# Attention and mixture of experts on one core: expert biases moved into the weights, and the softmax exponentials moved to ScalarE in front of the transposes

## The chip, the core and the metric

The kernel runs on one core of a Trainium2 chip. The core has five engines that run side by side, each through its own list of instructions in a fixed order: TensorE (PE, matmuls and transposes into PSUM), VectorE (DVE), ScalarE (ACT), GpSimd (POOL) and SyncE (SP, here an issuer of DMAs). They meet through semaphores. The metric is the device time of one execution in microseconds (us). Most executions of one kernel agree within 0.3%.

## What is computed

One transformer layer on x of shape 8 x 512 x 256 (eight batches), all in float32: causal attention with 16 heads of width 16, a layer norm, then a mixture of 16 experts of width 176 of which each token uses 6, and one shared expert of width 352, and a second layer norm.

```python
qkv = x @ w_qkv                                   # 16 heads of 16
scores = where(causal, q @ k.T / 4, -1e10)
x = layernorm(x + (softmax(scores) @ v) @ w_out)  # no gain, no offset
probs = softmax(x @ gate_w.T)
idx = top_k(probs + gate_b, 6);  c = probs at idx, else 0
y = sum over e of c[e] * ((silu(x @ w1[e].T + b1[e]) * (x @ w3[e].T + b3[e])) @ w2[e].T + b2[e])
z = (silu(x @ ws1.T + bs1) * (x @ ws3.T + bs3)) @ ws2.T + bs2
out = layernorm(x + y + z)
```

The layer norm has no learned gain or offset, so each row of what the experts read sums to zero up to rounding.

## The kernel before

The program is a list of steps ("line" in the code), and TensorE's instructions stand in exactly the order in which the steps write them; the other engines' order is chosen by the scheduler of the framework, by its own estimate of when things are ready, and is fixed in the program. Every step is a function `fn`, then what is `due` from earlier steps, then what is put `beside` it, then a function `behind`.

**Attention.** For a batch `transpose_x`, `project_qk` and `project_v` (L302 to L346) come first. Then there are 16 steps, one for each query tile q of 128 rows (q = 0 to 3), each half m of the heads, and each parity s. A step handles four heads (r = 0 to 3). `front` (L559) issues `scores` of step i and `turn_weights` of step i - 1; `back` (L566) issues `weighted_v` of step i - 2.

- `scores` (L348): TensorE computes four score tiles of 128 x (q+1)*128 into the four "sc" buffers of PSUM (L357). DVE adds the mask, scales by -0.25 and takes the row minimum of that, which is minus the row maximum, into `nb` (L368; a second short instruction reads the result out). GpSimd writes nb - e over e (L378), so that e holds score minus maximum.
- `turn_weights` (L384): for each key tile k up to q, TensorE transposes the four heads' 128 x 128 blocks into one "ps" buffer (L390), and ScalarE takes the exponential on the way to SBUF (L392, eT).
- `weighted_v` (L396): TensorE multiplies with v2 (L399). v2 holds, per pair of heads, v of the even head, sixteen ones, v of the odd head. A matmul of parity s thus gives, in 32 rows of `po`, sixteen rows of the weighted sum and sixteen of the row sum of the exponentials.
- `normalize` (L407), after both parities: ScalarE and DVE pick the two sums of even and odd heads apart with the masks `par`, a shuffle brings the sums to their partitions, DVE takes the reciprocal and multiplies (L414 to L426).

**Around it.** `finish_tokens` (output projection and layer norm), `transpose_tokens`, `gate` and `place` follow some steps later by `due`. `gate` leaves the routing weights in `cw` (L487); `place` transposes them into `cT` (L500, L501). `send` (L539) scatters token rows to the experts' slots with indirect DMAs that GpSimd issues. `shared_units` (L592) computes the shared expert of the batch before, beside the attention steps; its `collect` ends with a matmul of `cT` against `b2_sb`, which adds the routed b2 by weight and, through a column of ones, the shared bias (L636).

**Experts.** Batches form three groups (2, 4 and 2). `table` and `spread` (L650, L717) find which expert each tile of 128 routed rows belongs to. A unit of `expert_units` (L735) loads a tile of rows (`fetch`), transposes the next tile's rows and the hidden rows of two tiles before into one PSUM tile `tb` (`turn`; L780, L784; ScalarE copies xgT, L787, and hT, L791), multiplies with W1 and W3 of the expert (`up`, L799, `pab`), adds the two biases by one bf16 matmul (L806: a one-hot row `pick` of the tile's expert against `bparts`, each bias split into three bf16 parts by `split_biases`, L218), forms the gated hidden rows on ScalarE and DVE (L815 to L817), and multiplies with W2 (`down`, L826, `py`); ScalarE copies y (L834) and GpSimd issues the scatter of its rows (L835). The units of group 0 stand beside the attention of batches 2 to 6, those of group 1 beside batches 6 and 7 and after, those of group 2 at the end. `combine_units` (L865) adds a token's six rows on DVE and ends with the layer norm.

**Buffers.** PSUM has three pools: "sc" with four buffers, `po` with one, and "ps" with three, which the transposes of the weights, the projections, the gate, the shared expert, `tb`, `pab` and `py` all take in turn; a buffer is free again when its reader (mostly a copy by ScalarE) is done. In the last group every second tile of the units takes "sc" buffers. Loads and stores with fixed or register addresses are all issued by SP, in one order; three fills of spare slots with 2.2 MB each (`xs` from `none`) stand among them early on.

## Time and profile before

The times are 1665.35, 1656.8 and 1660.16 us, median 1660.16. The profile is of one execution, on the slowest core.

| | |
|---|---|
| profiled execution | 1653.36 us, span of the trace 1651.7 us |
| instructions | 30354 |
| mean granted TensorE clock | 0.931 |
| HBM | 75.61 MB read, 79.58 MB written, 94 GB/s |

| stage (us from the start) | PE busy | DVE | ACT | POOL | granted clock | DMA share |
|---|---|---|---|---|---|---|
| 9 to 108, batch 0 | 80.2 | 56.9 | 32.5 | 45.7 | 0.86 | 0.62 |
| 108 to 221, batch 1 | 99.4 | 68.7 | 38.4 | 68.6 | 0.86 | 0.12 |
| 221 to 341, batch 2 | 105.8 | 76.8 | 41.2 | 70.2 | 0.87 | 0.20 |
| 341 to 486, batch 3 | 134.6 | 80.4 | 59.0 | 85.4 | 0.96 | 0.19 |
| 486 to 635, batch 4 | 135.4 | 79.4 | 58.8 | 84.2 | 0.97 | 0.18 |
| 635 to 784, batch 5 | 135.2 | 83.6 | 60.2 | 87.6 | 0.97 | 0.19 |
| 784 to 951, batch 6 | 148.2 | 93.1 | 64.7 | 90.6 | 0.95 | 0.26 |
| 951 to 1197, batch 7 | 223.8 | 108.8 | 99.3 | 115.9 | 0.96 | 0.29 |
| 1197 to 1597, experts | 356.4 | 167.5 | 162.9 | 156.1 | 0.98 | 0.43 |
| 1597 to 1651, last sum | 0 | 31.6 | 0 | 5.1 | | 0.48 |

How to read it: "busy" is the time in us in which an engine ran instructions within the stage. A stage begins with the first q and k projection of its batch (L319). The granted clock is the share of full speed at which TensorE was let run. DMA share is the mean busy share of the core's 16 DMA engines. Lines such as "L378" are lines of the kernel file printed above; "out<-in" names the tiles; "<-" behind an idle time names what ended it. Ends of matmuls are modelled, so their starts are what to go by.

### The profile page before, as it was taken

The page shows a single profiled execution, that of the slowest core. Times are in us where ns is not written, and L with a number is a line of the kernel's source. Part 1 is how long each engine was busy: PE and PEld are TensorE (multiplying, and loading weights), DVE is VectorE, ACT ScalarE, POOL GpSimd, SP SyncE. Part 2 cuts the span into 40 slices and gives each one's busy share as a digit, 9 for nine tenths or more (in the row PEclk, how much of TensorE's full clock was granted, in tenths as well). Part 3 has the DMA queues.
Part 4 walks back from the last instruction along what each step waited for, and adds up shares of the span by engine and source line. Part 5 has one row for each costly group of instructions (what it writes and reads, how often), then busy time and mean ns, then how long its engine had stood idle before and what let it go on. Part 6 is the DMA issues. An engine that isn't in the chain of part 4 may idle for free.

```text
span 1651.7 us, 30354 instructions
## 1 busy us (share of the span) xinstructions
PE 1420.9 (86%) x9204; PEld 958.5 (58%) x9204; DVE 847.4 (51%) x3058; ACT 619.1 (37%) x1637; POOL 814.8 (49%) x1127
## 2 busy tenths in 40 slices
PE   7688998998999999899898998899888899888950
PEld 4454664665755566566555665566565666556740
DVE  4555756655645564556475534445343322675235
ACT  2232332343443343344343433444343343334520
POOL 4367565647465564746565435444545422343320
PEclk9787988998999999999999999999999999999985
DMA  9611102212121121211222324222233431785324
GB/s 259 195 42 41 47 35 92 60 57 67 55 67 54 44 67 47 71 46 63 69 85 72 91 74 134 71 81 84 69 103 103 130 97 45 228 242 163 97 89 131
DMA packets 147497, 151.37 MB, mean 92 GB/s; under 512 B 51215, under 2 KB 122499, under 8 KB 147338
## 3 DMA queue, kind: packets, MB, share of 16 engines
q1 hardware_dynamic: 126474, 96.69, 21.1%
q0 software_dynamic: 20592, 51.96, 8.6%
q8 instruction: 78, 1.28, 0.3%
q14 instruction: 81, 0.66, 0.1%
q10 hardware_dynamic: 272, 0.79, 0.1%
HBM read 75.61 MB, written 79.58 MB: 94 GB/s over the span
## 4 chain that ended last, share of the span: by engine, by line
PE 62%; DVE 14%; POOL 8%; issue 6%; DMA 5%; ACT 3%; another core or an unknown queue 1%; SPq 0%; POOLq 0%; DVEq 0%; ACTq 0%
PE pab L799 14%; PE py L826 10%; PE tp L390 7%; PE sc L357 5%; PE po L399 4%; DVE o L893 3%; PE qk L319 3%; DVE e L368 3%; PE pa L603 3%; PE tb L780 2%; POOL xs L543 2%; PE tb L784 2%; PE spy L629 2%; DMA o<-acc 2%; POOL e L378 2%
## 5 line engine op out<-in xcount | busy, mean ns | idle before, releaser
L835 POOL DMA_INDIRECT ys<-y,yat x237 | 239.1, 1009 | 336.0 <-ACT y L834 298.3
L799 PE MATMUL pab<-we_sb,xgT 128*128 x936 | 338.3, 485 | 14.8 <-DVE h L817 9.2
L378 POOL TENSOR_SCALAR e<-e,nb 128x512 f32<-128x512 f32 (+3 forms) x512 | 272.6, 544 | 156.9 <-DVE nb L368 143.0
L826 PE MATMUL py<-we_sb,hT 88*128 x948 | 252.8, 389 | 25.5 <-ACT hT L791 12.2
L392 ACT ACTIVATE eT<-tp 128x512 f32<-128x512 f32 x320 | 173.7, 599 | 269.0 <-PE tp L390 243.2
L368 DVE CUSTOM_DVE_ANT_0 e<-sc,none 128x512 f32<-128x512 f32 (+3 forms) x512 | 228.2, 479 | 53.7 <-PE sc L357 34.6
L390 PE MATMUL tp<-ident,e 128*128 128x128 f32 x1280 | 200.7, 300 | 49.7 <-POOL e L378 35.4
L826 PEld LDWEIGHTS py<-we_sb,hT 88*128 88x128 f32 x948 | 173.3, 195 | 98.2 <-issue 49.4
L816 DVE SCALAR_TENSOR_TENSOR h<-h,pab 128x176 f32<-128x176 f32 x237 | 79.4, 335 | 289.2 <-ACT h L815 242.5
L543 POOL DMA_INDIRECT xs<-x,idi x192 | 189.6, 987 | 76.9 <-issue 43.5
L390 PEld LDWEIGHTS tp<-ident,e 128*128 128x128 f32 x1280 | 151.1, 150 | 126.6 <-POOL e L378 68.3
L799 PEld LDWEIGHTS pab<-we_sb,xgT 128*128 128x128 f32 x936 | 165.2, 197 | 85.8 <-issue 19.4
L357 PE MATMUL sc<-kT,qT 32*128 32x384 f32 (+3 forms) x1024 | 140.2, 499 | 16.3 <-DVE nb L368 15.7
L815 ACT ACTIVATE h<-pab 128x176 f32<-128x176 f32 x237 | 75.3, 318 | 204.4 <-PE pab L806 165.8
L834 ACT COPY y<-py 128x256 f32<-128x256 f32 x237 | 88.3, 372 | 161.0 <-PE py L826 142.1
L787 ACT COPY xgT<-tb 128x256 f32<-128x256 f32 x234 | 87.2, 373 | 112.9 <-PE tb L784 76.9
L893 DVE SCALAR_TENSOR_TENSOR o<-yg,kept,o 128x256 f32<-128x256 f32 x192 | 94.3, 491 | 43.7 <-DMA o<-acc 23.3
L784 PE MATMUL tb<-ident,h 128*88 128x128 f32 x474 | 93.6, 280 | 19.4 <-DVE h L817 16.9
L780 PE MATMUL tb<-ident,xg 128*128 128x128 f32 x468 | 93.9, 283 | 16.2 <-DVE qT L328 8.9
L399 PE MATMUL po<-eT,v 128*32 128x128 f32 x2560 | 100.2, 283 | 1.5 <-DVE t L423 1.2
L357 PEld LDWEIGHTS sc<-kT,qT 32*128 32x128 f32 x1024 | 60.0, 192 | 58.1 <-DVE nb L368 29.4
L780 PEld LDWEIGHTS tb<-ident,xg 128*128 128x128 f32 x468 | 65.4, 148 | 43.4 <-issue 14.2
(161 smaller groups left out, 1741.4 us busy)
## 6 DMA issues: line engine op xcount, KB each, us to landing
xg<-xs SPq DMA_DIRECT2D x237, 128.0 KB
yg<-ys SPq DMA_DIRECT2D x96, 256.0 KB
we_sb<-in_w SPq DMA_DIRECT2D x6, 1408.0 KB
xs<-none SPq DMA_DIRECT2D x3, 2176.0 KB
xs<-none SPq DMA_DIRECT2D x48, 136.0 KB
x<-in_x SPq DMA_DIRECT2D x8, 512.0 KB
acc<-x SPq DMA_DIRECT2D x32, 128.0 KB
o<-acc SPq DMA_DIRECT2D x32, 128.0 KB
```

The costliest lines, as they stand in the source:

```text
L357: nc.tensor.matmul(sc[:, :n], lhsT=qT[ts(r, 32), m, s, ts(q, P)], rhs=kT[ts(r, 32), m, :n], start=True, stop=True,)
L368: nc.vector.tensor_tensor_reduce(out=e[:, :n], in0=scs[r][:, :n], in1=mask[:, S - n :], scale=-0.25, scalar=BIG, op0=ALU.add, op1=ALU.min, ...
L378: nc.gpsimd.tensor_scalar(e[:, :n], e[:, :n], -1.0, nb[:, r : r + 1], ALU.mult, ALU.add)
L390: nc.tensor.transpose(tp[:, ts(r, P)], es[r][:, ts(k, P)], ident)
L392: nc.scalar.activation(eT, tp, AF.Exp)
L399: nc.tensor.matmul(po[ts(r, 32), m, s, :], lhsT=v2[:, k, 4 * m + r, s : s + 2, :].rearrange("p h i -> p (h i)"), rhs=eTs[k][:, ts(r, P)], ...
L543: d = nc.gpsimd.indirect_dma_start(out=grp.xs, out_offset=bass.IndirectOffsetOnAxis(ap=idi[:, k : k + 1], axis=0), in_=xts[b][:, t, :], in ...
L780: nc.tensor.transpose(tp[:, c, :], xg[:, ts(c, P)], ident)
L799: nc.tensor.matmul(pab, lhsT=xgT[:, c, :], rhs=we_sb[:, ds(e * WE + c * 2 * EH, 2 * EH)], start=(c == 0), stop=False,)
L826: nc.tensor.matmul(py, lhsT=hT[:, c, :], rhs=we_sb[:HC, ds(e * WE + 4 * EH + c * D, D)], start=(c == 0), stop=(c == 1),)
L835: d = nc.gpsimd.indirect_dma_start(out=grp.ys, out_offset=bass.IndirectOffsetOnAxis(ap=st["at", j].bitcast(I32), axis=0), in_=y, in_offset ...
L893: nc.vector.scalar_tensor_tensor(o, y, kept[b][:, t, k : k + 1], o, ALU.mult, ALU.add)
```

## The change

Two things are changed.

First, the biases. The rows that the experts read sum to zero. Adding the same value to all 256 weights of a hidden unit therefore changes nothing. The copy of the transposed rows now adds one at feature 127 and at feature 255 (the last column of the identity matrix as a per-partition bias), so that the product gains the two weights at those features. `shifts` computes for each hidden unit half of (bias - weight 127 - weight 255) and stores it in DRAM, and `shift_weights` adds it to all weights of one expert, in place, for 16 experts in 16 consecutive steps. The matmul with `pick` and `bparts` and its preparation are gone. b2 goes into a row of the weights for the second product: hT keeps a row of ones behind its 88 rows, in two fixed tiles, and the last hidden tile of the shared expert, now one fixed tile, keeps a row of ones behind its 96. The matmul with `cT`, the tiles `cw` and `cT` and their transposes are gone.

Second, the softmax. GpSimd's subtraction is replaced by ScalarE's exponential with the maximum as bias, which also gives the row sums, before the transposes; the copy after the transposes is a plain one. v2 has zeros where it had ones, and both parities accumulate into the same 32 rows of `po`. The row sums' reciprocals are taken on DVE, spread over 16 columns by GpSimd (`over`), transposed by TensorE into the second half of `po`, copied by ScalarE (overT) and multiplied in by DVE.

```diff
+    nc.sync.dma_start(out=ws2_sb[LAST : LAST + 1, NHS - 1, :], in_=b2[E : E + 1, :])
...
+    nc.sync.dma_start(
+        out=wev[HC : HC + 1, :, 4 * EH + D :], in_=b2[:E, :].unsqueeze(0)
+    )
...
-    nc.gpsimd.memset(v2, 1.0)
+    nc.gpsimd.memset(v2, 0.0)
+    hTs = []
+    for i in range(2):
+        t = const.tile([P, 2, P], F32, tag=f"hT{i}", name=f"hT{i}")
+        nc.gpsimd.memset(t, 1.0)
+        hTs.append(t)
+    sh_last = const.tile([P, S], F32, name="sh_last")
+    nc.gpsimd.memset(sh_last, 1.0)
...
-    def split_biases():
+    def shifts():
...
-        for k in range(3):
-            part = three.tile([E, 2, EH], BF16, tag="h", name=f"part_{k}")
-            nc.vector.tensor_copy(part, rest)
-            if k < 2:
-                nc.vector.tensor_sub(rest, rest, part)
-            nc.sync.dma_start(
-                out=bparts[k * E : (k + 1) * E, :], in_=part.rearrange("e i n -> e (i n)")
-            )
+        lack = ten.tile([E, 2, EH], F32, tag="eT", name="lack")
+        nc.sync.dma_start(out=lack, in_=flats.rearrange("i (e n) -> e i n", e=E))
+        for c in range(ND):
+            have = three.tile([E, 2, EH], F32, tag="yg", name=f"have_{c}")
+            for i, w in enumerate((w1, w3)):
+                nc.sync.dma_start(
+                    out=have[:, i, :],
+                    in_=w[(c + 1) * P - 1, :HR].rearrange("(e n) -> e n", e=E),
+                )
+            nc.vector.tensor_sub(lack, lack, have)
+        nc.vector.tensor_scalar_mul(lack, lack, 0.5)
+        nc.sync.dma_start(out=shift, in_=lack.rearrange("e i n -> e (i n)"))
+
+    def shift_weights(e):
+        c = three.tile([P, 2 * EH], F32, tag="yg", name=f"shift_{e}")
+        nc.sync.dma_start(out=c, in_=shift[e].partition_broadcast(P))
+        w = wev[:, e, : 4 * EH].rearrange("p (c n) -> p c n", c=ND)
+        nc.vector.tensor_add(w, w, c.unsqueeze(1).to_broadcast([P, ND, 2 * EH]))
...
-                nc.gpsimd.tensor_scalar(
-                    e[:, :n], e[:, :n], -1.0, nb[:, r : r + 1], ALU.mult, ALU.add
+                nc.scalar.activation(
+                    e[:, :n],
+                    e[:, :n],
+                    AF.Exp,
+                    bias=nb[:, r : r + 1],
+                    scale=-1.0,
+                    accum_out=sums[:, m, r, s : s + 1],
                 )
                 es.append(e)
+            if s == 1:
+                over = two.tile([P, P], F32, tag="over", name=f"over_{b}_{q}_{m}")
+                nc.vector.reciprocal(sums[:, m], sums[:, m])
+                nc.gpsimd.tensor_copy(
+                    over.rearrange("p (r s i) -> p r s i", s=2, i=HD),
+                    sums[:, m].unsqueeze(3).to_broadcast([P, 4, 2, HD]),
+                )
+                done["over", q, m] = over
...
-                nc.scalar.activation(eT, tp, AF.Exp)
+                nc.scalar.copy(eT, tp)
...
-                        po[ts(r, 32), m, s, :],
+                        po[ts(r, 32), 0, m, :],
...
-                        start=(k == 0),
-                        stop=(k == q),
+                        start=(s == 0 and k == 0),
+                        stop=(s == 1 and k == q),
...
-                nc.scalar.mul(a, po[:, i, :], par[:, 1:2])
...
-            nc.vector.scalar_tensor_tensor(
-                t[0], po[:, 1, :], par[:, 0:1], t[0], ALU.mult, ALU.add
-            )
-            nc.vector.stream_shuffle(den, t[0], SWAP)
-            nc.vector.reciprocal(den, den)
-            nc.vector.scalar_tensor_tensor(
-                t[1], po[:, 0, :], par[:, 0:1], t[1], ALU.mult, ALU.add
-            )
-            nc.vector.tensor_mul(aT[:, m, :], t[1], den)
+            nc.tensor.transpose(po[:, 1, m, :], done.pop(("over", q, m)), ident)
+            over = two.tile([P, P], F32, tag="overT", name=f"overT_{b}_{q}_{m}")
+            nc.scalar.copy(over, po[:, 1, m, :])
+            nc.vector.tensor_mul(aT[:, m, :], po[:, 0, m, :], over)
...
-            nc.vector.tensor_mul(cw[:, :E], sel, pb)
...
-            nc.tensor.transpose(pc, cw, ident)
-            nc.scalar.copy(cT[:, ts(t, P)], pc)
...
-            nc.tensor.matmul(
-                py, lhsT=cT[:, ts(t, P)], rhs=b2_sb, start=False, stop=True
-            )
...
-                nc.scalar.copy(xgT, tp[:, :ND, :])
+                nc.scalar.activation(
+                    xgT, tp[:, :ND, :], AF.Identity, bias=ident[:, P - 1 :]
+                )
...
-            nc.tensor.matmul(
-                pab,
-                lhsT=grp.pick[:, j : j + 1].to_broadcast([P, P]),
-                rhs=bparts,
-                start=False,
-                stop=True,
-            )
...
-                    lhsT=hT[:, c, :],
-                    rhs=we_sb[:HC, ds(e * WE + 4 * EH + c * D, D)],
+                    lhsT=hT[: HC + c, c, :],
+                    rhs=we_sb[: HC + c, ds(e * WE + 4 * EH + c * D, D)],
...
-    put(10, split_biases)
+    put(10, shifts)
+    for e in range(E):
+        put(14 + e, lambda e=e: shift_weights(e))
```

## The prediction

> **What bounds the kernel now.** I read the page's busy rows, then the waits of TensorE, then the groups by line, then the timeline of single steps. The first view is the page: engines over the span, the granted clock in 40 slices, the chain of work that ended last.

> ```profile
> PE 1420.9 (86%) x9204; PEld 958.5 (58%) x9204; DVE 847.4 (51%) x3058; ACT 619.1 (37%) x1637; POOL 814.8 (49%) x1127
> ...
> PEclk9787988998999999999999999999999999999985
> ...
> PE 62%; DVE 14%; POOL 8%; issue 6%; DMA 5%; ACT 3%; another core or an unknown queue 1%; SPq 0%; POOLq 0%; DVEq 0%; ACTq 0%
> ```

> TensorE is the bound: it is busy 1421 of the 1597 us before its last instruction, and ScalarE is hardly on the chain (3%). The windows of the trace split the span: batches 0 to 2, 9 to 341 us, almost without expert units (TensorE busy 86%, clock 0.86); batches 3 to 6, 341 to 951 us, with 0.8 units a step (91%, 0.96); batch 7, to 1197 us, with three; some 115 units alone, to 1597 us; a last sum of 54 us without TensorE. The first of TensorE's waits by length (who, for whom: us in total, times, longest), and the groups of ScalarE by shape (busy us, mean ns | idle before):

> ```profile
> PE tp L390 <- POOL e L378: 35.4, 32, 4.9
> ```

> ```profile
> L392 ACT ACTIVATE eT<-tp 128x512 f32<-128x512 f32 x320 | 173.7, 599 | 269.0 <-PE tp L390 243.2 <-remote 13.5 <-PE pa L603 6.1
> ...
> L414 ACT ACTIVATE t<-po,par 128x128 f32<-128x128 f32 x128 | 40.1, 364 | 61.7 <-PE po L399 31.1 <-PE qk L319 13.7 <-PE tp L390 6.8
> ...
> L612 ACT ACTIVATE sha<-pa,hbs 128x512 f32<-128x512 f32 x16 | 11.0, 688 | 17.7 <-PE pa L603 16.7 <-issue 1.1
> ```

> The subtraction on GpSimd holds the transposes up for 35 us of TensorE's idle time. A ScalarE pass with a per-partition operand (688 ns, 364 ns at 128 columns) costs more than one without (599 ns). The timeline of one step of the last query tile (q = 3) in batch 4 (start, length), first TensorE, then ScalarE, then the read of the step's first row maximum on DVE, is the measure for all that follows:

> ```profile
> 602.83 1.14 PE L357 MATMUL sc<-kT,qT 32*128 32x512 f32 x8
> 603.90 2.06 PE L390 MATMUL tp<-ident,e 128*128 128x128 f32 x16
> 605.80 0.43 PE L445 MATMUL x1p<-ident,x 128*128 128x128 f32 x2
> 606.28 0.44 PE L780 MATMUL tb<-ident,xg 128*128 128x128 f32 x2
> 606.55 0.38 PE L784 MATMUL tb<-ident,h 128*88 128x128 f32 x2
> 606.88 1.45 PE L799 MATMUL pab<-we_sb,xgT 128*128 x4
> 608.17 0.31 PE L806 MATMUL pab<-bparts,pick 128*128 128x352 bf16 x1
> 609.73 1.13 PE L826 MATMUL py<-we_sb,hT 88*128 x4 [1.24 <-issue]
> 610.79 0.86 PE L399 MATMUL po<-eT,v 128*32 128x128 f32 x24
> ```

> ```profile
> 604.65 2.18 ACT L392 ACTIVATE eT<-tp 128x512 f32<-128x512 f32 x4 [2.14 <-PE tp L390]
> 606.90 0.37 ACT L448 COPY x1T<-x1p 128x256 f32<-128x256 f32 x1
> 609.03 0.37 ACT L787 COPY xgT<-tb 128x256 f32<-128x256 f32 x1 [1.76 <-PE pab L806]
> 609.30 0.37 ACT L791 COPY hT<-tb 88x256 f32<-88x256 f32 x1
> ```

> ```profile
> 604.60 0.08 DVE L368 DVE_READ_ACCUMULATOR2_ANT nb<- 128x1 f32 x1
> ```

> TensorE runs scores, the transposes of the step before, a unit, the weighted sum. ScalarE answers each transposed block at once (0.53 us apart), so the three "ps" buffers come free as fast as TensorE fills them; GpSimd's work on this step's scores stands in no one's way before the next step.

> **Part 1, the biases.** Removed on TensorE: 237 bias matmuls L806; in the pure expert stage the next matmul follows 0.15 us later, 237 x 0.15 = 36 us where TensorE is the limit. The 32 shared bias pairs L636 (0.44 us from 592.62 to 593.06) give 14 us, the 32 transposes L500 0.14 us each, 4 us. DVE's product L487 and ScalarE's copy L501 go with them, hidden now by TensorE. The wider contractions (89 for 88 rows, 97 for 96) stream the same columns: nothing. The copy xgT gains a per-partition bias, by the rows above 0.09 us: 21 us of ScalarE, in the pure expert stage covered by about 0.4 us between the end of hT and the matmuls that read it.

> Added, once: one chain of DMAs and 16 adds of 128x704 on DVE. By 422 ns for 256 columns and 704 for 512 an add is 0.9 us, 14.6 us in all, inside batch 0's q = 3, where DVE is busy about 65% and has some 13 us free in 40. The SP queue gets 23 transfers more (four for "have", one "shift", 16 reads of 360 KB, two of bias rows) and loses four; the 5.8 MB take 18 us at the 320 GB/s of 50 to 60 us, in a stage that is 2 to 13% busy after 70 us. DVE today waits 12.5 us there for the flattened bias (TensorE 11.9 us behind it). That wait stays; the read now stands ahead of the first 2.2 MB fill (7 us at that rate, at most won), while the reads of "shift" stand behind two fills and a store (14 us and more lost, with every row maximum queued behind the add). I take +8, bounds -7 and +25.

> **Part 2, exponentials on ScalarE.** GpSimd loses 512 passes (273 us) and gets 64 copies "over" (about 0.39 us, the row of 128x128). DVE loses two products, shuffle and reciprocal for each of 64 normalizations (0.35 + 0.34 + 0.30 + 0.95 us, 124 us in all). Both are hidden today except those 35 us. TensorE gets 64 transposes (0.14 us, 9 us). Two waits are new: on GpSimd "over" waits for DVE's reciprocal, with scatters queued behind it that no engine waits for within a stage; on ScalarE the copy overT waits for its transpose, with the next exps behind it, 0.3 us at most as it follows the weighted sum at once.

> ScalarE gets 512 passes with a per-partition bias and a sum. Length: 364 ns at 128 columns and 688 at 512; passes in a row overlap by 0.07 (four of 599 ns in 2.18 us); the read of a sum adds 0.09 to 0.19 us (after the gate's exp at 618.63 the next copy starts at 618.90). I take 0.09, as the starts show it: 0.38, 0.49, 0.60, 0.71 us for q = 0 to 3, 279 us (with 0.19: 330). ScalarE goes to some 620 + 279 + 21 - 49 + 17 = 890 us, 54%: not a bound by its sum.

> Its order is what costs. In the changed program a step's ScalarE work stands as exp, exp, exp of this step, the copy of the first transposed block of the step before, the last exp, the other copies, then xgT and hT. So the copies that free "ps" wait for exps that wait for row maxima of this very step. At q = 3, from the start of the scores: first maximum at 1.85 us (604.68 in the timeline), three exps from 1.95 to 4.08, first copy to 4.61, last exp to 5.32, copies to 5.85, 6.37, 6.90. The fourth block can be transposed only at 4.7, the transposes x1p at 5.95, the unit's at 6.45, pab at 7.05, py at 8.3, the weighted sum ends at 9.95: against 8.75 in the trace. The neighbours by the same steps: 9.7 against 8.0, 10.15 against 10.1. I take +1.0 a step at q = 3, +1.0 at q = 2 (8.6 against about 7.5), +0.6 for the two q = 1 steps without shared work, +0.3 at q = 0: 10.4 us a batch, the saved L806 included.

> Without a unit the same wait holds the fourth transposed block: 1.95 + 2.13 + 0.53 + 0.1 + 0.5 + 0.9 = 6.1 us from scores to scores at q = 3, plus some 0.7 of other matmuls, against 5.3 in batch 1: +1.5 a step. At q below 3 ScalarE needs 4.4 us at most, under the 4 to 6 of today's steps: nothing; if that cover failed, 0.5 us a step, 18 us.

> **The sum,** against the profiled run (1653.4 us, span 1651.7): batches 0 to 2, 12 x 1.5 + 8 = +26; batches 3 to 6, 4 x 10.4 = +42; batch 7, 10.4 less 32 more units at 0.15, +5; pure expert stage, 115 x 0.15 + 4 x 0.44, -19; last sum, 0. Together +54: 1707. The median of the runs shown is 7 us above the profiled run: **1714 us**.

> [...] In the trace TensorE's clock falls with its gaps: after 11.9 us idle, eight score matmuls took 3.07 us instead of 0.93, and the windows 50 to 70 us show 0.63 and 0.52. [...]

> **Rivals.** *Faster, the stalls find cover.* TensorE's work falls by 36 + 14 + 4 - 9 = 45 us and GpSimd's 35 us of waits end: 1580 at best, some 1620 when half of the stalls remain. For it: ScalarE idle 63%, and TensorE's present waits before py (1.24 us above) may be the same microseconds. Against: the fixed order. It decides if the first transposes of a unit at q = 2 and 3 start within 0.5 us of TensorE's work before them. 24%. *The clock goes too.* If the steps of batches 3 to 7 drop from 0.96 to 0.86, their 777 us of busy TensorE grow by up to 12%, 90 us; as the gaps fill only part of each step I take half: 1760, at most 1804, 12%. *Both signs cancel,* 1652 to 1668: 7%. That the exponentials do not move can be excluded: the built program has them on ScalarE ahead of the transposes.

> **How the numbers follow.** The forecast has 57%, by itself 1670 to 1760. The measurement tells 0.5% from no change, 1652 to 1668: faster 24%, same 7%, slower 57 + 12 = 69%. The range 1620 to 1785 leaves out the fast rival's better half and the end of the clock's.

> **What will show it.** Right: TensorE's waits in attention name eT or e on ScalarE, more than 100 us together, where they named GpSimd; q = 3 steps near 10 us in batches 4 and 5; a unit in the pure expert stage 0.15 us shorter; ScalarE 860 to 940 us busy. Wrong: batches 3 to 6 no longer than today's 145 to 167 us (the ScalarE order costs nothing), or an exp of 512 columns well off 0.7 us.

## The result, and the profile after

The changed kernel takes **1775.69 us** (median; 1772.39 to 1795.31), the kernel before 1661.64 us in the same comparison: a ratio of **1.07** (95% interval 1.0621 to 1.0778), 114 us slower. The forecast was slower by 54 us, 1714 us, with a range of 1620 to 1785: direction and range held, the size was half of what came.

The profiled execution took 1795.31 us (span 1793.6), the longest of its runs. A second profile, taken later beside other versions, has a span of 1766.9 us and stands nearer the median; where it matters both are given. The page of the first:

```profile
PE 1438.7 (80%) x8932; PEld 955.8 (53%) x8932; DVE 760.4 (42%) x2773; ACT 883.4 (49%) x2565; POOL 561.1 (31%) x678
...
PEclk8788989898978988898889999899978999999995
...
PE 55%; ACT 15%; DVE 11%; issue 8%; DMA 5%; POOL 2%; another core or an unknown queue 2%; SPq 1%; DVEq 0%; POOLq 0%; ACTq 0%
```

TensorE runs 272 matmuls less (8932 for 9204) and is busy for 18 us more. The last row is the chain that ended last: ScalarE's share went from 3% to 15%, GpSimd's from 8% to 2%. The granted clock, 9 before from slice 11 on, has 7s and 8s all through the attention. TensorE's longest waits (who, for whom: us, times, longest):

```profile
PE tp L410 <- ACT eT L412: 63.0, 29, 6.5
PE spy L634 <- ACT eT L412: 35.4, 21, 2.5
PE pab L797 <- ACT eT L412: 24.9, 10, 6.0
PE pb L606 <- ACT eT L412: 23.1, 16, 6.0
PE py L817 <- ACT hT L789: 22.3, 25, 5.0
PE cnt L504 <- ACT eT L412: 21.0, 8, 4.4
```

The 35 us on GpSimd are gone, as forecast, and whatever stands behind a transposed block on TensorE, its next block (tp), the shared expert (spy, pb), a unit (pab), the gate (cnt), now waits for ScalarE's copy eT, 167 us in five rows. What stands in front of that copy is seen in one step of ScalarE, the one whose scores start at 662.65 us (start, length):

```profile
664.62 0.72 ACT L384 ACTIVATE e<-e,nb 128x512 f32<-128x512 f32 x1 [1.60 <-DVE nb L374]
...
665.35 0.71 ACT L384 ACTIVATE e<-e,nb 128x512 f32<-128x512 f32 x1
...
666.05 0.71 ACT L384 ACTIVATE e<-e,nb 128x512 f32<-128x512 f32 x1
...
666.76 0.56 ACT L412 COPY eT<-tp 128x512 f32<-128x512 f32 x1
667.22 0.72 ACT L384 ACTIVATE e<-e,nb 128x512 f32<-128x512 f32 x1
...
667.94 1.04 ACT L412 COPY eT<-tp 128x512 f32<-128x512 f32 x2
```

Three exponentials of this step, then one copy of the step before, the last exponential, the other copies: the order that the prediction had read from the program. ScalarE idles 1.60 us on the first row maximum (it starts 1.97 us after the scores, 1.95 predicted) while the finished blocks stand in PSUM. TensorE in this step and the next:

```profile
663.72 1.53 PE L410 MATMUL tp<-ident,e 128*128 128x128 f32 x12
667.37 0.40 PE L504 MATMUL cnt<-sel,before 128*128 128x16 f32 x2 [2.12 <-ACT eT L412]
...
668.83 1.96 PE L797 MATMUL pab<-we_sb,xgT 128*128 x4
670.58 1.91 PE L817 MATMUL py<-we_sb,hT 88*128 x4
...
673.39 1.14 PE L363 MATMUL sc<-kT,qT 32*128 32x512 f32 x8
674.46 1.53 PE L410 MATMUL tp<-ident,e 128*128 128x128 f32 x12
680.89 1.11 PE L410 MATMUL tp<-ident,e 128*128 128x128 f32 x4 [4.89 <-ACT eT L412]
...
683.47 2.56 PE L797 MATMUL pab<-we_sb,xgT 128*128 x4
685.82 1.37 PE L817 MATMUL py<-we_sb,hT 88*128 x4
```

Three blocks fill the three "ps" buffers, then TensorE stands: 2.12 us, and in the next step 4.89 (this one has a second cause, told further down). After that gap four matmuls `pab` take 2.56 us, where the step shown of before has 1.45 for them. The windows of the trace say why (from:to and length, then TensorE's busy time with its instructions, the granted clock, DMA share, GB/s): first batches 3 to 6 as a whole, then this stretch in pieces of 3.41 us. All 117 changes of the clock in this trace lie multiples of 3.413 us apart; the pieces shown are cut 0.2 us ahead of them, which gives the 0.53 and 0.97:

```profile
365.00:1078.00 713.00, 581.35 (x3875) 0.90 0.18 55
...
665.80:669.21 3.41, 1.49 (x10) 1.00 0.00 0
669.21:672.63 3.42, 3.42 (x12) 0.53 0.27 79
672.63:676.04 3.41, 3.36 (x44) 0.97 0.33 123
676.04:679.45 3.41, 0.00 (x0) 1.00 0.16 57
679.45:682.87 3.42, 1.91 (x8) 0.53 0.11 41
682.87:686.28 3.41, 3.41 (x10) 0.50 0.16 39
```

The two pieces with little work at full clock (1.49 and 0.00 us of it) are each followed by one at 0.53, the first although the gap in it was only 2.12 us. So both stalls, 2.12 and 4.89 us, are paid for twice: by their length, and by the matmuls behind them (`pab` takes 1.96 and 2.56 us for 1.45).

Batches 3 to 6 (from the first projection of batch 3 to that of batch 7) in the versions, all worked out from the traces, in us. "Beside scatters" is the part of TensorE's idle time that lies in a row of GpSimd's indirect DMAs or up to 2 us behind it (a row: at most 0.4 us between them, over 3 us in all; these stretches fill 154 to 182 us of each version). "Half" counts the pieces of 3.41 us that ran at half clock. The versions are told of below.

| version | length | TensorE busy | idle | of it beside scatters | half | of |
|---|---|---|---|---|---|---|
| before | 609.2 | 552.6 | 56.6 | 31.3 | 14 | 178 |
| changed, first profile | 712.7 | 581.0 | 131.7 | 50.9 | 42 | 208 |
| changed, second profile | 688.5 | 559.9 | 128.6 | 49.2 | 28 | 201 |
| bias part alone | 609.7 | 547.2 | 62.5 | 32.3 | 23 | 178 |
| all exponentials ahead of the copies | 719.6 | 580.0 | 139.6 | 49.0 | 43 | 210 |
| two ahead (fourth set) | 640.5 | 550.2 | 90.3 | 45.8 | 23 | 187 |
| two ahead (third set) | 592.7 | 532.9 | 59.9 | 11.7 | 13 | 173 |
| all behind hT | 620.1 | 548.1 | 71.9 | 45.9 | 21 | 181 |
| spread (fourth set) | 605.7 | 543.9 | 61.8 | 46.5 | 20 | 177 |
| softmax part alone, spread (fourth set) | 608.0 | 556.3 | 51.8 | 41.3 | 18 | 177 |
| softmax part alone, spread (third set) | 549.3 | 533.8 | 15.5 | 3.7 | 3 | 160 |
| four "ps" buffers, three "sc" | 687.6 | 602.0 | 85.5 | 39.1 | 32 | 200 |
| transposes of group 2 fourfold | 689.6 | 589.1 | 100.4 | 48.7 | 20 | 201 |

The two profiles of the changed kernel are worth a look: the same program has nearly the same idle time, 131.7 and 128.6 us, and differs by 21.1 us of busy time; 14 half-speed pieces of 3.41 us at half their length are 23.9. What lies between them is almost the clock alone.

### The profile page after: what moved, and what is told of

The parts are those of the page before. It is cut to its first block, busy times and chain, and to the rows that moved or that the text cites. A ratio compares the mean times of both kernels' runs of the same rounds, so it can differ in the third digit from the quotient of the medians.

```text
span 1793.6 us, 29831 instructions
## 1 busy us (share of the span) xinstructions
PE 1438.7 (80%) x8932; PEld 955.8 (53%) x8932; DVE 760.4 (42%) x2773; ACT 883.4 (49%) x2565; POOL 561.1 (31%) x678
## 4 chain that ended last, share of the span: by engine, by line
PE 55%; ACT 15%; DVE 11%; issue 8%; DMA 5%; POOL 2%; another core or an unknown queue 2%; SPq 1%; DVEq 0%; POOLq 0%; ACTq 0%
PE pab L797 14%; PE py L817 10%; ACT e L384 10%; PE sc L363 5%; PE po L420 5%; ACT eT L412 3%; DVE e L374 3%; PE qk L322 3%; PE tp L410 3%; PE tb L776 3%; PE tb L780 2%; DVE o L884 2%; PE spy L634 2%; PE pb L606 2%
## 5 line engine op out<-in xcount | busy, mean ns | idle before, releaser
L797 PE MATMUL pab<-we_sb,xgT 128*128 x936 | 356.8, 507 | 37.5 <-ACT eT L412 24.9
L384 ACT ACTIVATE e<-e,nb 128x512 f32<-128x512 f32 (+3 forms) x512 | 282.7, 553 | 201.8 <-DVE nb L374 168.6
L826 POOL DMA_INDIRECT ys<-y,yat x237 | 237.5, 1002 | 427.0 <-ACT y L825 383.7
L817 PE MATMUL py<-we_sb,hT 88*128 (+1 forms) x948 | 264.8, 403 | 25.0 <-ACT hT L789 22.3
L817 PEld LDWEIGHTS py<-we_sb,hT 88*128 88x128 f32 (+1 forms) x948 | 186.2, 203 | 112.0 <-ACT hT L789 61.1
L410 PE MATMUL tp<-ident,e 128*128 128x128 f32 x1280 | 190.7, 295 | 65.0 <-ACT eT L412 63.0
L410 PEld LDWEIGHTS tp<-ident,e 128*128 128x128 f32 x1280 | 148.6, 149 | 140.3 <-ACT eT L412 72.7
L412 ACT COPY eT<-tp 128x512 f32<-128x512 f32 x320 | 170.2, 575 | 20.5 <-remote 11.5
L783 ACT ACTIVATE xgT<-tb,ident 128x256 f32<-128x256 f32 x234 | 110.6, 473 | 115.9 <-PE tb L780 74.9
L806 ACT ACTIVATE h<-pab 128x176 f32<-128x176 f32 x237 | 75.1, 317 | 149.6 <-PE pab L797 129.7
L363 PE MATMUL sc<-kT,qT 32*128 32x384 f32 (+3 forms) x1024 | 127.5, 546 | 1.7 <-DVE nb L374 1.7
L780 PE MATMUL tb<-ident,h 128*88 128x128 f32 x474 | 97.5, 289 | 21.0 <-DVE h L808 14.5
L420 PE MATMUL po<-eT,v 128*32 128x128 f32 x2560 | 110.9, 303 | 2.8 <-issue 2.2
L384 ACT ACTIVATION_READ_ACCUMULATOR e<-e,nb 128x1 f32 x512 | 95.7, 187 | 0.0
```

What stands on the lines that cost most here:

```text
L363: nc.tensor.matmul(sc[:, :n], lhsT=qT[ts(r, 32), m, s, ts(q, P)], rhs=kT[ts(r, 32), m, :n], start=True, stop=True,)
L384: nc.scalar.activation(e[:, :n], e[:, :n], AF.Exp, bias=nb[:, r : r + 1], scale=-1.0, accum_out=sums[:, m, r, s : s + 1],)
L410: nc.tensor.transpose(tp[:, ts(r, P)], es[r][:, ts(k, P)], ident)
L412: nc.scalar.copy(eT, tp)
L420: nc.tensor.matmul(po[ts(r, 32), 0, m, :], lhsT=v2[:, k, 4 * m + r, s : s + 2, :].rearrange("p h i -> p (h i)"), rhs=eTs[k][:, ts(r, P)], ...
L780: nc.tensor.transpose(tp[:HC, 2 + c, :], h[:, ts(c, HC)], ident)
```

## The experiments

The theory after the result: the loss is the place of the exponentials in ScalarE's queue, and its price is TensorE's idle time and the half-speed pieces that follow. The rivals: the softmax part costs by its work, wherever it stands; or the few PSUM buffers are at fault; or the clock fell for a reason of its own. Four sets were run, each against the kernel before on the same chip: it took 1663.16 us in the first set, 1666.98, 1596.26 and 1651.48 in the others, so ratios are compared, and across sets with care. The record names chip 9 for the first, 11 for the second and 13 for the third and the fourth.

**The two parts alone.** First the kernel before with the bias part only.

> The kernel before with the bias part of the change alone (attention as before). If the loss comes from the order on ScalarE (the theory), this part keeps its gain: 237 bias matmuls, 32 pairs and 32 transposes gone, 16 adds and 0.09 us a unit on ScalarE new, so 1625 to 1652 us against 1662. If the added chain of weight shifts or the longer xgT copy costs as much as it saves, 1655 to 1680.

Measured: 1637.26 us, ratio 0.9845 (0.9826 to 0.9864). Then the softmax part only.

> The kernel before with the softmax part of the change alone (biases as before). Theory: the whole loss and the bias matmuls on top, 1785 to 1825 us. If both parts share the loss, 1700 to 1770.

Measured: 1816.16 us, ratio 1.0925 (1.0895 to 1.0955). So the bias part gains 26 us, and the softmax part, in the order that the scheduler chose, loses 153. Of the bias part's 26 us, 12 lie in the stage of the experts alone (397.4 to 385.5); batches 3 to 6 did not get shorter (609.2 to 609.7) although they lost bias matmuls: in the profile of this version TensorE idles 6 us more there (62.5 for 56.6), and 23 pieces run at half clock for 14. The work taken away came back as idle time and as a slower clock.

**Order alone.** The changed kernel, instruction for instruction, with ScalarE's order written out: the copies of the transposes, xgT and hT, then the four exponentials, then tanh and y.

```diff
+            def exps():
+                for r, e in enumerate(es):
+                    nc.scalar.activation(
...
+            pending.append(exps)
...
             st["hT", j - 2] = hT
+            flush()
...
-    with tc.manual_schedule(engines={ET.PE}):
+    with tc.manual_schedule(engines={ET.PE, ET.Activation}):
```

> The changed kernel with the same instructions, but ScalarE's order written out: the copies of the transposed blocks, then xgT and hT of the step's first unit, then the four exponentials. Theory (copies that free the PSUM buffers queue behind exponentials that wait for this step's row maxima): the waits of TensorE for eT shrink from some 130 us to under 40 and the clock comes back, 1600 to 1670 us. Rival (ScalarE's 280 us more work, or the sums' reads, are the cost wherever they stand): 1740 to 1790.

Measured: 1646.95 us, ratio 0.9905 (0.9884 to 0.9926), 129 us under the changed kernel by medians. The rival that the work itself costs this loss falls. The control is the other fixed order, the lines of the changed kernel as they are written, with all four exponentials ahead of every copy:

> The changed kernel with ScalarE's order fixed as its lines are written: all four exponentials of a step ahead of every copy of transposes, in place of the scheduler's mixed order. A control for the version whose order is also fixed but with the exponentials last. If the place of the exponentials sets the time (theory), this is the worst order: 1790 to 1840 us, with the waits of tp behind eT longer than the changed kernel's 63 us. If fixing the order as such was what helped, it comes near the other fixed version: 1640 to 1700.

Measured: 1816.15 us (1802.24 to 1818.04), ratio 1.0862 (1.0789 to 1.0935). Fixing the order isn't what helped; the place of the exponentials is. The idle time away from the scatters follows that place: 90.6 us with all ahead, 80.8 and 79.4 in the changed order, 44.5 and 48.2 with two ahead, 26.0 with all behind hT and 15.3 spread, for 25.3 before.

**Where TensorE's repeats are free.** Here the transposes of one group are issued four times into the same place, so that TensorE has work where it waited. First the transposes of the last or third group in all steps with q of 1 or more (96 steps), then only those of the third group, k = 2 (64 steps, shown):

```diff
-                for r in range(4):
+                for r in 4 * list(range(4)) if k == 2 else range(4):
                     nc.tensor.transpose(tp[:, ts(r, P)], es[r][:, ts(k, P)], ident)
```

> The changed kernel with the transposes of the third key block (the second at q = 1) done four times over into the same buffer, 12 more transposes or 1.5 us of TensorE work in 96 steps, just ahead of the wait for the copies. If the gaps cost clock too, TensorE stays at full clock behind the wait and the time falls although work is added: 1720 to 1765 us, mean clock 0.93 or more. If the clock has no part in it, the added work only fills idle time or lengthens steps that have none: 1775 to 1830, clock as before.

Measured: 1788.61 us, ratio 1.0752 (1.073 to 1.0773): in the rival's range, with the clock up (0.928 in the profile, 0.895 in that of the changed kernel). Alone this decided nothing, since it also put work into short steps that had no wait to hide it (batches 0 to 2 took 369 us for 356).

> The changed kernel with the transposes of group 2 issued four times into the same place, in place of once: 64 steps with some 1.5 us of TensorE work more, 96 us in all, placed at a spot where TensorE waits. If the idle gaps themselves cost the clock (theory), filling them gives most of the lost clock back: granted clock .93 or above in batches 3 to 6, and 1735 to 1765 us in spite of the work. If the gaps cost only their own length and the clock has other causes, the repeats fill waits at best and lengthen the rest: 1775 to 1815.

Measured: 1774.71 us, ratio 1.0653 (1.0615 to 1.069). The time is unchanged, above the range of the theory (1735 to 1765) and at the lower edge of the rival's. But 768 transposes more, 78 us of TensorE's busy time by the groups (268.6 for 190.7 us), cost nothing. The profile says what paid for them:

```profile
374.00:1063.00 689.00, 588.59 (x4246) 0.95 0.18 57
```

This is the window of batches 3 to 6, to be set against the first row of the windows of the changed kernel above: 371 more recorded matmuls in 7 us more of busy time, at a clock of 0.95 for 0.90. Against the second profile it is 29 us more of busy time at 0.95 for 0.93, with 28 us less idle. Without the transposes L410, TensorE's records in that stretch cover 468.6 us for 499.4 and 480.0, the same work. So filling gaps does bring the clock back, in all four runs of this version (0.923 to 0.927 over the whole run, 0.895 to 0.912 in the nine of the changed kernel); the repeats then used it up. That speaks against a clock that fell for a reason of its own; how much of the 114 us it is worth is read below, from idle and busy time.

**More buffers.** One PSUM buffer moved from "sc" (4 to 3) to "ps" (3 to 4):

> The changed kernel with one PSUM buffer moved from the pool of the scores (4 to 3) to the general pool (3 to 4), which holds tp and the products behind it: TensorE may then run one tile further before it waits for a copy on ScalarE. If the waits come from the few buffers (theory: they are freed by copies that stand behind exponentials), each is put off by one tile: 1700 to 1750 us. If the wait is for the data (eT must be copied before the product that reads it), or the scores now lack their fourth buffer, nothing is won: 1765 to 1800.

Measured: 1747.64 us, ratio 1.0473 (1.0421 to 1.0525), at the top of the theory's range. The waits on eT nearly go, and a new one comes:

```profile
PE sc L363 <- DVE nb L374: 109.3, 120, 5.9
```

Now the scores wait for their buffer, 109 us. Depth moves the wait; it takes about a third of the loss away, the order all of it.

**A better order, and the dose.** In the fixed order with the exponentials last, tanh still stood behind all four, and `pab` waited for y (16.9 us), `tb` for the hidden rows (19.8). The spread order puts rows 0 and 1 behind hT, row 2 behind tanh, row 3 behind y:

```diff
+            pending.extend(lambda r=r: exp(r) for r in range(4))
...
             st["hT", j - 2] = hT
+            flush(2)
...
             nc.scalar.activation(h, pab[:, :EH], AF.Tanh, scale=0.5)
+            flush(1)
```

> The changed kernel with ScalarE's order written out, and the four exponentials of a step spread out instead of standing together: the copies of the transposes, xgT and hT first, then the exponentials of rows 0 and 1, tanh, the exponential of row 2, y, the exponential of row 3. The theory (what an instruction on ScalarE costs is set by what TensorE work stands queued behind it, and the step as a whole has room on ScalarE) expects the waits that the version with all four exponentials ahead of tanh still has (pab behind y 16.9 us, tb behind the h of VectorE 19.8) to shrink by half or more, and 1610 to 1645 us, below that version's 1647. Rival: the last exponential now comes one instruction before the next step's transposes, which need it, so the wait only moves there; then 1645 to 1680.

Measured: **1632.45 us**, ratio **0.9782** (0.9742 to 0.9823): faster than the kernel before. The wait on y is gone from the list; that on the hidden rows stayed at 18.5 us, so that step of the expectation missed. Two in between are a dose: rows 0 and 1 ahead of the copies, 2 and 3 behind hT; and the kernel before with the softmax part alone in the spread order.

> The changed kernel with ScalarE's order written out, the exponentials of rows 0 and 1 ahead of the copies of the transposes and those of rows 2 and 3 behind hT. A dose between the fixed orders with none ahead (1647 us) and all four ahead (1817). Theory (each exponential ahead of the copies adds its own wait for its row maximum and its own length to TensorE's wait): about the middle, 1700 to 1760. Rival (one early exponential is already enough, as the copies then wait for this step's scores at all): 1770 to 1820. Other rival (only the last one or two matter, as the first are done while TensorE transposes): 1640 to 1680.

> The kernel before with the softmax part alone, its exponentials in the order spread behind the copies (copies of the transposes, xgT, hT, rows 0 and 1, tanh, row 2, y, row 3). The softmax part alone took 1816 us in the scheduler's order, and the bias part alone saves 26 of the 1663 us before. Theory (the whole loss is the order, and what the softmax part does otherwise is small): 1640 to 1665 us, so that bias part and softmax part in this order add up to the 1632 measured for both. Rival: the softmax part has a cost of its own that the bias part's saving hides in that run: 1670 to 1710.

Measured: 1576.63 us (ratio 0.9909, 0.9874 to 0.9944) and 1531.4 us (ratio 0.9597, 0.9577 to 0.9617), but in a set in which the kernel before took 1596.26 us. These can't be set beside the others, so both were run again with the changed kernel and the spread order in one set.

> The softmax part alone on the kernel before, in the spread order, now on the same chip as the other three of this set. On a chip where the kernel before takes 1596 us it gave a ratio of 0.960; the version with both parts in that order gave 0.978 on a chip where before takes 1667. If the difference is the chip's, the ratio here goes with the chip and lies 0.010 to 0.020 ABOVE that of the version with both parts (the bias part's own saving, 0.0155, is missing from it). If the softmax part alone is really the better one, because the bias part takes TensorE work out of steps that wait anyway and lengthens xgT, its ratio is equal or lower: by 0 to 0.015.

> Both parts, exponentials in the spread order, on the same chip as the other three of this set. Where the two parts add, it is the fastest of the four: 0.010 to 0.020 below the softmax part alone in this order. Where the bias part gives nothing in the stages with attention, it stands within 0.010 of it, and only the expert stage at the end is shorter, by 10 to 14 us (the bias part alone took that stage from 397 to 385 us).

> The changed kernel with rows 0 and 1 ahead of the copies and rows 2 and 3 behind hT, on the same chip as the changed kernel itself and the spread order. It gave a ratio of 0.991 on another chip. Theory (each early exponential adds its own wait): about the middle between the spread order and the changed kernel. Other rival (the first two are done while TensorE transposes, and only the last ones cost): within 0.010 of the spread order.

> The changed kernel itself on the same chip as the other three. If the loss is the order of ScalarE's queue alone, the ratio to before is 1.06 to 1.08 on any chip. If the first measurement leaned on the chip it ran on, it is off by more: below 1.05 on a chip where the kernel before is at 1596 us.

The record gives this set and the third the same chip, number 13, so the "another chip" of these expectations is not borne out; what differs between the two sets is told in the last section.

| fourth set, before 1651.48 us | us | ratio (95% interval) |
|---|---|---|
| both parts, spread order | 1618.9 | 0.9799 (0.9766 to 0.9833) |
| softmax part alone, spread order | 1637.49 | 0.9889 (0.9853 to 0.9924) |
| both parts, two exponentials ahead | 1677.18 | 1.013 (1.0094 to 1.0165) |
| both parts as changed | 1765.94 | 1.0675 (1.0635 to 1.0715) |

In one set the two parts add, less a little: 0.009 between the first two rows, where the bias part alone gave 0.0155 (0.010 to 0.020 was expected, so just missed); in their profiles the experts' stage alone is 14 us shorter (394.7 to 380.8). The softmax part is a gain of 14 us (65 in the third set) once its exponentials stand behind the copies. The changed kernel's ratio stayed in its range, 1.06 to 1.08. Two early exponentials cost 58 us, the changed order 147 against the spread one; the middle between the two would be 1692, so the later exponentials cost more than the first two. TensorE's waits in the spread order (fourth set) show what is left:

```profile
PE tp L419 <- ACT e L393: 17.5, 43, 2.3
PE tb L790 <- DVE h L820: 14.3, 11, 3.4
PE py L829 <- ACT hT L799: 12.2, 16, 1.7
```

And ScalarE in one of its steps, the third of q = 3 in batch 4, whose scores started at 602.30 us:

```profile
604.07 2.06 ACT L421 COPY eT<-tp 128x512 f32<-128x512 f32 x4 [1.17 <-PE tp L419]
...
606.65 0.47 ACT L793 ACTIVATE xgT<-tb,ident 128x256 f32<-128x256 f32 x1
607.00 0.36 ACT L799 COPY hT<-tb 88x256 f32<-88x256 f32 x1
607.25 0.73 ACT L393 ACTIVATE e<-e,nb 128x512 f32<-128x512 f32 x1
...
609.58 0.36 ACT L837 COPY y<-py 128x256 f32<-128x256 f32 x1
609.83 0.74 ACT L393 ACTIVATE e<-e,nb 128x512 f32<-128x512 f32 x1
```

All four blocks are copied within 2.06 us as they come, as in the kernel before (2.18 us), and the first three exponentials, 607.25 to 609.59, stand beside TensorE's work at the unit and at the weighted sum (606.21 to 609.56). Its next scores start at 609.49, 7.2 us after these; the same step takes 12.9 and 10.1 us in the two profiles of the changed kernel and 10.1 in the kernel before.

## Why the prediction was right, and where it was wrong

**The mechanism was right.** The order in ScalarE's queue, the first exponential at +1.95 us (1.97), the wait at the fourth block, the waits' names (eT; "more than 100 us", 167 came): all as worked out. ScalarE is busy 883 us (890 predicted). The shapes of the exponential:

```profile
L384 ACT ACTIVATION_READ_ACCUMULATOR e<-e,nb 128x1 f32 x512 | 95.7, 187 | 0.0
L384 ACT ACTIVATE e<-e,nb 128x512 f32<-128x512 f32 x128 | 91.4, 714 | 78.8 <-DVE nb L374 70.9 <-issue 3.8 <-DVE bi L479 3.8
...
L384 ACT ACTIVATE e<-e,nb 128x384 f32<-128x384 f32 x128 | 77.6, 607 | 55.9 <-DVE nb L374 51.5 <-DVE mv_a L259 3.7 <-DVE sel L493 0.6
```

One of 512 columns takes 714 ns (the figure behind the busy time in the second row); in the step shown the starts lie 0.70 to 0.73 us apart with the read of the sum between, 0.71 predicted. That the change does not do what it says was rightly excluded, and the fast rival (the stalls find cover) did not come for this order; it came, with 33 us, for the spread one. Of the signs, "q = 3 steps near 10 us in batches 4 and 5" came in part: 10.1 to 12.7 us in the second profile for those with a unit, up to 14.8 in the first.

**Term by term,** against the profile of before (span 1651.7), for the second profile of the changed kernel (1766.9), whose difference of 115 us is that of the medians:

| | predicted | second profile | first profile |
|---|---|---|---|
| batches 0 to 2 | +26 | +24 | +24 |
| batches 3 to 6 | +42 | +79 | +104 |
| batch 7 | +5 | +16 | +26 |
| experts alone | -19 | -5 | -12 |

The sum of the first row holds, in part by luck: in batches 1 and 2 the steps at q = 3 grew by 1.0 us where 1.5 were worked out and those at q = 2 by 0.8 to 1.0 where nothing was, and those at q = 1 became 0.8 to 1.0 us shorter. **The step that failed is the second: "10.4 us a batch"; 19.8 were measured** (25.9 in the first profile). By q = 0 to 3 its steps grew by 0.5, 0.6, 1.6 and 2.5 us in the second profile, on average (at q = 3 without the fourth step, which holds the next batch's projections), where 0.3, 0.3, 1.0 and 1.0 had been put.

The forecast's 42 us were some 57 us of stalls less about 15 of removed matmuls (13 units at 0.15 and four shared pairs at 0.44 us a batch). Counted at full clock (half of the busy time in half-speed pieces left out), TensorE's work there fell by 14 us, as forecast. Its idle time grew by 72 us, 15 more than forecast, and what the half-speed pieces cost grew by 21 us, from 20 to 41, where the forecast had nothing. Together this is the 37 us that were lacking. In the first profile 62 were: 18 idle time and 43 clock.

Why the idle time was too low: not shown to be the price of the order. Away from the scatters it grew by 54 us (56 in the first profile), near the 57 of the forecast. Beside them it grew by 18 (20), and there every version with the softmax part has 39 to 51 us outside the third set, whatever the order, for 31 before. The step of the changed kernel that starts at 673.39 shows what happens there. It takes 14.8 us for 9.95, and begins at full clock. TensorE's four scores end at 674.51 to 674.53 by its records. VectorE and ScalarE, and below them GpSimd with its scatters, at the same time:

```profile
675.92 0.69 DVE L374 CUSTOM_DVE_ANT_0 e<-sc,none 128x512 f32<-128x512 f32 x1 [4.04 <-PE tp L410]
...
677.36 0.69 DVE L374 CUSTOM_DVE_ANT_0 e<-sc,none 128x512 f32<-128x512 f32 x1 [0.73 <-PE tp L410]
...
679.50 0.69 DVE L374 CUSTOM_DVE_ANT_0 e<-sc,none 128x512 f32<-128x512 f32 x1 [0.83 <-remote]
...
680.25 0.58 ACT L412 COPY eT<-tp 128x512 f32<-128x512 f32 x1 [0.58 <-remote]
```

```profile
674.10 0.96 POOL L546 DMA_INDIRECT xs<-x,idi  x1 [0.30 <-issue]
675.36 0.96 POOL L546 DMA_INDIRECT xs<-x,idi  x1 [0.30 <-issue]
676.63 1.00 POOL L826 DMA_INDIRECT ys<-y,yat  x1 [0.30 <-issue]
677.93 0.97 POOL L546 DMA_INDIRECT xs<-x,idi  x1 [0.30 <-issue]
```

VectorE takes the first score 1.4 us and the last 5.0 us after its end, the exponentials wait for the row maxima, and the copy of the first block, which ended at 675.12, starts at 680.25 behind three of them. The same step, the second of q = 3 in batch 4, takes 14.9 us with all exponentials behind hT and 14.5 in the spread order too, and 7.3 and 8.8 us in the two profiles of the third set. So its length is not the order's doing. At 662.65, where the inputs came as the forecast had taken them, the step took 10.7 us for 9.7, of which `pab` and `py` at half clock are 1.3 (3.87 us for 2.58 in the step shown of before).

Why the clock was counted as nothing: that the stalls cost none was the author's estimate, by which the sum has no term for it, and no run shows it. Behind the stall of 2.12 us shown above the clock was 0.53, and half-speed pieces cost 21 us more than before in the second profile and 43 in the first. The clock was told as a rival ("the clock goes too", 1760, 12%), and that is where more than half of the missing time went (21 of 37 us, 43 of 62). Cut where the trace's clock changes, every piece of 3.41 us in batches 3 to 6 has a clock of 0.50 or 1.00: 14 and 164 in the profile of before, 42 and 166 in the first of the changed kernel.

**The stage of the experts** gave 12 us for the 19 with the bias part alone (385.5) and in the first profile (385.8), 5 in the second (392.2), all for 397.4 before: at most 0.09 us for each of 115 units, rather than the 0.15 after which the next matmul had followed. The copy xgT got longer by 0.10 us (473 for 373 ns), as predicted; that its cover failed in part is one reading, and no run tells this.

What the 16 adds of 128x704 cost on VectorE (886 ns each, 0.9 predicted) and the SP queue's reads can't be told apart from the rest of batches 0 to 2, whose sum was right; taking them out alone wasn't tried. Batch 7 (+16 and +26 for +5) was not taken apart.

## What to carry to other kernels

Before a pass is moved to an engine with room, read what stands behind it in that engine's queue: here the same instructions took 1766 us in the order that a scheduler had chosen and 1619 us in one written out, with the copies that free TensorE's buffers first and the exponentials, needed only a step later, in the slots where the engine waits anyway. Price a stall of TensorE by its length and by the half-speed work that follows it (here 72 us more of idle time and 21 us more for half-speed pieces in batches 3 to 6), and look whether the same stall comes back in every step. And where steps end on waits, work removed from the waiting engine can be worth little: without the bias matmuls batches 3 to 6 took 609.7 us for 609.2, and in the spread order 605.7 for 608.0.

## What was not expected of the hardware

**How little it takes to halve TensorE's clock.** In the sixteen profiles, batches 3 to 6 were cut into pieces of 3.41 us where each trace's clock changes. What followed a piece at full clock, by TensorE's busy time in it:

| busy in a full-speed piece | pieces | next piece at half clock |
|---|---|---|
| under 1.4 us | 141 | 141 |
| 1.4 to 2.0 us | 137 | 52 |
| 2.0 to 2.5 us | 218 | 30 |
| over 2.5 us | 2131 | 6 |

**Results of TensorE that arrive late beside scatters.** VectorE's wait for a score and ScalarE's for a transposed block can be timed: how long after the end of TensorE's record does the reader start, when it stood idle? In fourteen profiles the median of 2247 such waits is some 38 ns, but 498 readers start more than 0.3 us late, up to 7.9. At 496 of these GpSimd was issuing an indirect DMA when TensorE's record ended, or had been less than 1.5 us before; so it was at 1006 of the 1749 that were on time. In the kernel before 12 of 190 are late, in the versions with the softmax part 25 to 52 of 89 to 239. In the two profiles of the third set it is none of 291, though 197 are near a scatter. So the scatters alone don't do it, and what else it takes is open; so is whether TensorE itself ended late or only the news of it, as its ends are modelled. The two traces of the third set hold nearly all of TensorE's semaphore updates (2567 of 2567 and 2467 of 2471), the fourteen others 92 to 95%, so a part of the recording in it is not excluded.

**The same file, 1531.4 and 1637.49 us.** This is where the two sets part. The softmax part alone in the spread order had, in batches 3 to 6 of the third set's profile, 15.5 us of idle time and 3 half-speed pieces of 160; in the fourth set's 51.8 us and 18 of 177, with ScalarE and VectorE equally busy (857 and 859, 748 and 749 us over the span). Beside scatters lie 3.7 and 41.3 us of that, elsewhere 11.8 and 10.5. The loss by order is there in both sets: with two exponentials ahead TensorE idles 48.2 us away from the scatters in the third and 44.5 in the fourth. The changed kernel itself has no run in the third set, so how much slower it is without late results wasn't measured.
